# LayerNorm's inverse roots: a GpSimd power and one Newton step on VectorE in place of ScalarE's square root and VectorE's reciprocal

## The chip, the cores and the metric

The kernel runs on one core of a Trainium2 chip. The metric is the device time of one execution in microseconds (us), the median of several runs. The core's engines work side by side, each through its own queue in order: TensorE (PE, with PEld for its weight loads), VectorE (DVE), ScalarE (ACT), GpSimd (POOL) and SyncE (SP, which here only issues DMAs). An engine waits for another through semaphores.

## What is computed

Two pre-LayerNorm layers act on x of 4 x 1024 tokens by 256 features, all in float32. Cut to what matters:

```
def _layernorm(x, eps=1e-05):
    return (x - mean(x)) / sqrt(var(x) + eps)          # over the 256 features

x = x + L0_attn(_layernorm(x))    # causal attention in a window of 64, 16 heads
x = x + L0_ffn (_layernorm(x))    # top 2 of 8 SwiGLU experts, and 2 shared experts
x = x + L1_attn(_layernorm(x))    # full attention; inside it, after the output projection:
                                  #   out = out + input
                                  #   out = (out - mu) * rsqrt(var + 1e-05) * gamma + beta
x = x + L1_ffn (_layernorm(x))    # 8 experts choose 128 tokens each, gates by 8 Sinkhorn rounds
```

So every token has five normalisations: four of the layers, and the one inside the second attention. Each needs one number per token, 1/sqrt(var + eps).

## The kernel before

**Tiles.** A tile is 128 tokens (on the partitions) by 256 features. The 32 tiles `x_t[i]` stay in SBUF from start to end. A unit `u` is four tiles (`UT` = 4), `NT` = 32.

**Statistics and roots.** `note(i)` computes mean and variance of tile i on VectorE (`bn_stats`, `bn_aggr`) into `mv_all[:, i, :]`. `roots(i0, i1)` (L140 to L144) then turns the variances of several tiles at once into inverse roots: ScalarE takes the square root of variance plus epsilon (L143, one column per tile), VectorE the reciprocal (L144), and the result lies in `rstd_all`. ScalarE's functions are kept in tables; a change from a function of one table to one of another shows in the trace as an instruction ACT_TABLE_LOAD. ScalarE computes the softmax exponentials (L378 in layer 0, L1479 in layer 1), the SwiGLU's silu (L725) and plain copies beside the square roots.

**Where roots are taken.**
- At the start for tiles 0 to 3 and 4 to 7, then inside the projection of layer 0 for tiles 8 to 19 (about 31 us) and 20 to 31 (about 235 us). `normalise_steps` uses them in L157 (VectorE), and TensorE transposes the normalised tile `xn` in L164. GpSimd is at the start busy with memsets of the q, k and v buffers (L236, L239, L298).
- For all 32 tiles at the start of layer 0's FFN (about 475 us). In program order GpSimd has there DMA issues (L547, L549, L590, L595), iotas, masks and memsets down to L762, and after them L597, which waits for a DMA.
- For layer 1's attention, for tiles 0 to 3 (about 1204 us), 4 to 11 (about 1268 us) and 12 to 31 (about 1422 us, at the end of `fetches`, which brings the experts' rows back). L1331 in `project` and L1528 in `put_out` use them.
- In `finish` (L1540 and after), ten times, for the inner LayerNorm of one to four tiles (seven times four, then two, one and one): statistics of `y`, root (L1552), reciprocal, then GpSimd applies scale, gamma and beta and adds the result to x (L1559 and after). `note` follows.
- In `gate_steps` (L1014 and after), ten times for the same groups: root (L1017), reciprocal, then GpSimd normalises a tile for the second FFN (L1024), TensorE transposes it and computes gate logits, which VectorE clips (L1055).

**Layer 1's attention loop.** From about 1330 to 2330 us TensorE works step by step. One step computes transposed scores of a head pair into a double PSUM bank (L1471; of its four matmuls two subtract the rows' maxima), scores for later maxima into another (L1429), and sums over values for an earlier step (L1486). ScalarE takes the exp of the first (L1479, 1.02 us) and VectorE the maxima of the second (L1436, 1.2 us). These double banks are one ring of three buffers in turn: a score matmul waits until the exp or the reduction of three buffers earlier has read its buffer.

**Order.** What lies beside the loop (output projections, `finish`, projections of later units, gates, Sinkhorn, choosing tokens, rank DMAs) is written as Python generators. The loop calls `some`, which advances each kind of job by a piece; a `yield 0` or `wait(lag)` in a job gives its turn away, so that other instructions of the same engines come between. The scheduler keeps these instructions behind the newest of the loop's own. `paced` ties GpSimd's fetch DMAs to a ScalarE instruction. The tail after the loop finishes the last tiles with `lag` 0, chooses tokens for the remaining sequences and runs the experts (to 2504 us).

Of the kernel before, what the change touches and what calls it, by code (L numbers as in the profile page):

```python
# [8 lines left out]
F32 = mybir.dt.float32  # L9
# [4 lines left out]
AF = mybir.ActivationFunctionType  # L14
ALU = mybir.AluOpType
# [3 lines left out]
P = 128  # L19
# [3 lines left out]
NT = NB * S // P  # L23
UT = 4
# [9 lines left out]
EPS = 1e-5  # L34
# [5 lines left out]
def two_layers(  # L40
# [33 lines left out]
    nc = tc.nc  # L74
    mm = nc.tensor.matmul

    const = ctx.enter_context(tc.tile_pool(name="const", bufs=1))
    small = ctx.enter_context(tc.tile_pool(name="small", bufs=3))
# [24 lines left out]
    for i in range(NT):  # L103
# [6 lines left out]
    make_identity(nc, ident)  # L110
    identb = const.tile([P, P], BF16, tag="identb", name="identb")
    make_identity(nc, identb)
    eps_t = const.tile([P, 1], F32, tag="eps", name="eps_t")
    nc.vector.memset(eps_t, EPS)

    dsel = const.tile([P, P], F32, tag="dsel", name="dsel")
    nc.gpsimd.memset(dsel, 0.0)
# [1 line left out]
        out=dsel,  # L119
# [12 lines left out]
    mv_all = const.tile([P, NT, 2], F32, tag="mv_all", name="mv_all")  # L132
    rstd_all = const.tile([P, NT], F32, tag="rstd_all", name="rstd_all")

    def note(i: int):
        st = small.tile([P, 6], F32, tag="st", name="st")
        nc.vector.bn_stats(st, x_t[i])
        nc.vector.bn_aggr(mv_all[:, i, :], st)

    def roots(i0: int, i1: int):  # L140

        std = small.tile([P, NT], F32, tag="std", name="std")
        nc.scalar.activation(std[:, i0:i1], mv_all[:, i0:i1, 1], AF.Sqrt, bias=eps_t)  # L143
        nc.vector.reciprocal(rstd_all[:, i0:i1], std[:, i0:i1])  # L144

    def normalise(*args, **kw):
        for _ in normalise_steps(*args, **kw):
# [30 lines left out]
    with ExitStack() as lc:  # L178
# [7 lines left out]
            out=wv_t, in_=w_qkv[:, 2 * D :].rearrange("(k p) e -> p k e", p=P)  # L186
# [3 lines left out]
        with tc.tile_pool(name="a0_raw", bufs=1) as rpool:  # L190
            for n in range(2):
                w_raw = rpool.tile([P, 2, D], F32, name=f"w_raw{n}")
                nc.scalar.dma_start(
                    out=w_raw,
# [3 lines left out]
                for kc in range(2):  # L198
                    for j in range(2):
                        half = slice(j * P, (j + 1) * P)  # L200
# [12 lines left out]
            out=mask_q, in_=mask_q, compare_op=ALU.is_ge, fill=NEG,  # L213
# [3 lines left out]
            out=mask_q, in_=mask_q, compare_op=ALU.is_ge, fill=NEG,  # L217
# [7 lines left out]
            out=spread.rearrange("p (r c) -> p r c", r=4)[:, :, :DH],  # L225
# [8 lines left out]
        for n in range(2):  # L234
# [3 lines left out]
            k = wpool.tile([P, 4, S], F32, name=f"kT{n}")  # L238
# [309 lines left out]
    for b in range(NB):  # L548
        nc.gpsimd.dma_start(  # L549
            out=y_d[b][E * CAP :, :].rearrange("o (p n) -> (o p) n", p=4), in_=none[:4, :]  # L550
# [11 lines left out]
    with ExitStack() as lc:  # L562
# [16 lines left out]
        for n in range(PAIRS):  # L579
            order.append((2 * n, 2, n))  # L580
            if (n + 1) * (NBLK - PAIRS) // PAIRS > n * (NBLK - PAIRS) // PAIRS:
                n = PAIRS + n * (NBLK - PAIRS) // PAIRS
# [181 lines left out]
        for r in range(0, NTILE, 12):  # L764
            n = min(12, NTILE - r)
# [244 lines left out]
    def wait(n: int):  # L1010
        for _ in range(n):
            yield 0

    def gate_steps(i0: int, i1: int, bank, lag: int):  # L1014

        std = small.tile([P, NT], F32, tag="std", name="std")
        nc.scalar.activation(std[:, i0:i1], mv_all[:, i0:i1, 1], AF.Sqrt, bias=eps_t)  # L1017
        yield from wait(lag)
        nc.vector.reciprocal(rstd_all[:, i0:i1], std[:, i0:i1])
        yield from wait(lag)  # L1020
        xns = []
        for t in range(i0, i1):
            xn = gpool.tile([P, D], F32, tag="xng", name="xng", bufs=4)
            nc.gpsimd.tensor_scalar(  # L1024
                xn, x_t[t], mv_all[:, t, 0:1], rstd_all[:, t : t + 1], ALU.subtract, ALU.mult
            )
            nc.gpsimd.dma_start(out=xn_d[t // TB][(t % TB) * P : (t % TB + 1) * P, :], in_=xn)
            xns.append(xn)
            yield 0
        yield from wait(2 * lag)  # L1030
        xTs = []
        for j in range(0, i1 - i0, 2):
            pair = xns[j : j + 2]
            ps = bank()
            for h, xn in enumerate(pair):
                for kc in range(2):
                    c = (2 * h + kc) * P
                    nc.tensor.transpose(ps[:, c : c + P], xn[:, kc * P : (kc + 1) * P], ident)
            xT = gpool.tile([P, 4, P], F32, tag="xTg", name="xTg")
            n = 2 * len(pair)  # L1040
            nc.scalar.copy(xT[:, :n, :].rearrange("p k t -> p (k t)"), ps[:, : n * P])
            xTs += [xT[:, 2 * h : 2 * h + 2, :] for h in range(len(pair))]
            yield 1
        yield from wait(lag)
        ps = bank()
        for j, xT in enumerate(xTs):
            for kc in range(2):
                mm(
                    ps[:, j * E : (j + 1) * E],
                    lhsT=xT[:, kc, :],  # L1050
                    rhs=gw1[:, kc, :],
                    start=(kc == 0),
                    stop=(kc == 1),
                )
        nc.vector.tensor_scalar(  # L1055
            gates[:, i0:i1, :],
            ps[:, : (i1 - i0) * E].rearrange("p (j e) -> p j e", e=E),
            CLIP,
            None,
            ALU.max,  # L1060
        )
        yield 1
# [191 lines left out]
    with ExitStack() as lc:  # L1254
# [285 lines left out]
        def finish(i0: int, ys):  # L1540

            n = len(ys)
            lag = 2 if i0 + n < NT else 0
            mv = small.tile([P, 4, 2], F32, tag="mv1", name="mv1")
            for j in range(n):
                st = small.tile([P, 6], F32, tag="st", name="st")
                nc.vector.bn_stats(st, ys[j])
                nc.vector.bn_aggr(mv[:, j, :], st)
                yield 0
            yield from wait(lag)  # L1550
            std = small.tile([P, 4], F32, tag="std1", name="std1")
            nc.scalar.activation(std[:, :n], mv[:, :n, 1], AF.Sqrt, bias=eps_t)  # L1552
            yield from wait(lag)
            rstd = small.tile([P, 4], F32, tag="rstd1", name="rstd1")
            nc.vector.reciprocal(rstd[:, :n], std[:, :n])
            yield from wait(lag)
            for j in range(n):
                x = x_t[i0 + j]
                nc.gpsimd.tensor_scalar(  # L1559
                    ys[j], ys[j], mv[:, j, 0:1], rstd[:, j : j + 1], ALU.subtract, ALU.mult  # L1560
                )
                nc.gpsimd.tensor_tensor(ys[j], ys[j], gamma_b, ALU.mult)
                nc.gpsimd.tensor_tensor(ys[j], ys[j], beta_b, ALU.add)
                nc.gpsimd.tensor_tensor(x, x, ys[j], ALU.add)
                yield from wait(lag)
            yield from wait(2 * lag)
            for j in range(n):
                note(i0 + j)
                yield 0
            yield from wait(lag)  # L1570
            gating.append(gate_steps(i0, i0 + n, misc_bank, 2 if lag else 0))
            if i0 + n == GT:
                gating.append(share_steps(0, misc_bank, 2))
                gating.append(then(lambda: sort.append(
                    choose_steps(0, misc_bank, chosen, chose)
                )))
# [108 lines left out]
        def fetches():  # L1685

            note_some()
            yield 0
            for i, k in to_fetch:
                fetch(i, k, newest["scalar"])  # L1690
                yield from wait(2)
                take(2)
                note_some()
            yield from wait(4)
            take(0)
            note_some()
            roots(3 * UT, NT)

        def stacks():
            roots(0, UT)  # L1700
# [188 lines left out]
```

## Time and profile before

| | |
|---|---|
| runs | 2508.35, 2501.3, 2497.42 us; median 2501.3 |
| profiled execution | 2505.83 us |
| its span, from the first to the last instruction | 2504.1 us |
| mean granted TensorE clock | 0.955 of full speed |
| ScalarE's table loads | 50 in all, 1.283 us each |
| ScalarE's square roots | 28, about 0.30 us each |

The page gives each engine's busy time and its share of the span; then the span in 40 slices of 62.6 us, each digit being the busy share of a slice in tenths; then groups of instructions (line, engine, operation, output and input, count, busy us, mean ns, idle us of the engine before them and who ended most of it). In the timeline a row gives start and length in us, engine, line, operation, tiles and shapes; a bracket at its end gives the engine's idle time before it and who released it. A row of waits gives the waiting engine and line, who released it, the sum in us, how many times, and the longest.

### The profile page before, as it was taken

How to read it: one execution, taken by the hardware profiler on the slowest of the kernel's cores; microseconds unless marked ns; L12 is line 12 of the kernel's file. 1: busy time of each engine (PE TensorE's matmuls, PEld its weight loads, DVE VectorE, ACT ScalarE, POOL GpSimd, SP SyncE). 2: the span in 40 equal slices, each digit the busy share in tenths (PEclk: the TensorE clock that was granted, in tenths of full speed). 3: DMA queues.
4: the chain of work that ended last, by engine and by line, in shares of the span. 5: the costliest groups of instructions: out<-in, count | busy, mean ns of one | idle time of the engine just before them, and what ended most of it. 6: DMA issues, size and time to landing. Idle time of an engine off the chain costs nothing.

```text
span 2504.1 us, 42234 instructions
## 1 busy us (share of the span) xinstructions
PE 2273.6 (91%) x16844; PEld 1352.2 (54%) x16844; DVE 1392.9 (56%) x2304; ACT 985.6 (39%) x1354; POOL 632.2 (25%) x728
## 2 busy tenths in 40 slices
PE   6999999799999999999888999999999999998434
PEld 3566666566557888887444444444444444443222
DVE  5455545524321222222476877777777798995393
ACT  1333333312111222222114666666666565666311
POOL 2233333510440000000333221212122211124455
PEclk8999999899999999999999999999999999999667
DMA  3000000420116666664515221313121313100144
GB/s 93 19 11 11 11 13 9 133 74 1 66 63 200 217 206 209 213 207 156 117 44 120 59 69 45 69 45 69 45 69 45 69 44 69 44 19 11 56 122 135
DMA packets 201744, 204.90 MB, mean 82 GB/s; under 512 B 90200, under 2 KB 162392, under 8 KB 201548
## 3 DMA queue, kind: packets, MB, share of 16 engines
q1 hardware_dynamic: 179148, 162.13, 22.7%
q0 software_dynamic: 11584, 29.72, 4.0%
q10 hardware_dynamic: 10816, 10.36, 1.2%
q8 instruction: 133, 2.18, 0.4%
q14 instruction: 63, 0.52, 0.1%
HBM read 140.70 MB, written 56.96 MB: 79 GB/s over the span
## 4 chain that ended last, share of the span: by engine, by line
PE 69%; DVE 16%; issue 6%; ACT 4%; POOL 3%; DMA 3%; SPq 0%; DVEq 0%; ACTq 0%; POOLq 0%
PE two L962 10%; PE two L1471 9%; PE acc L1486 8%; PE two L717 6%; DVE tops L1436 5%; PE two L329 5%; PE two L1429 4%; PE acc L989 4%; PE two L258 3%; PE two L1351 2%; PE two L321 2%; PE acc L735 2%; PE misc L735 2%; PE acc L396 2%; PE misc L440 1%
## 5 line engine op out<-in xcount | busy, mean ns | idle before, releaser
L1436 DVE TENSOR_REDUCE tops<-two 128x2 f32<-128x1024 f32 x512 | 619.5, 1217 | 103.8 <-PE two L1429 101.6
L1479 ACT ACTIVATE pT<-two 128x1024 f32<-128x1024 f32 x512 | 523.4, 1025 | 303.7 <-PE two L1471 299.2
L1486 PE MATMUL acc<-pT,v_t 128*32 128x256 f32 x4096 | 342.7, 393 | 5.8 <-ACT pT L1479 5.6
L1471 PE MATMUL two<-q_st,k_st 64*128 64x512 f32 x1024 | 259.8, 499 | 19.3 <-ACT pT L1479 11.8
L962 PE MATMUL two<-xbT,w_t 128*128 128x256 f32 (+1 forms) x1280 | 260.0, 358 | 1.3 <-ACT xbT L951 0.7
L717 PE MATMUL two<-xnT_f,w_t 128*128 128x512 f32 x512 | 234.7, 608 | 7.4 <-DVE tops L1436 5.1
L962 PEld LDWEIGHTS two<-xbT,w_t 128*128 128x128 f32 x1280 | 224.1, 192 | 32.0 <-ACT xbT L951 5.3
L1429 PE MATMUL two<-k_st,q_st 64*128 64x512 f32 x1024 | 220.3, 403 | 4.2 <-DVE glu L726 1.6
L1471 PEld LDWEIGHTS two<-q_st,k_st 64*128 64x128 f32 x1024 | 96.8, 184 | 209.8 <-issue 118.8
L1659 POOL DMA_INDIRECT yr<-ys_d,slot x64 | 62.6, 979 | 573.5 <-DMA w_raw<-in_L_attn_wk_dram 434.7
L1471 PE MATMUL two<-top_st,minus 64*128 64x512 f32 x1024 | 206.5, 396 | 0.0
L978 DVE SCALAR_TENSOR_TENSOR glu_b<-two,b_blk,act_b 128x256 f32<-128x256 f32 (+1 forms) x160 | 72.6, 453 | 235.8 <-ACT act_b L972 235.8
L972 ACT ACTIVATE act_b<-two,b_blk 128x256 f32<-128x256 f32 (+1 forms) x160 | 72.1, 451 | 312.6 <-PE two L962 161.1
L1486 PEld LDWEIGHTS acc<-pT,v_t 128*32 128x32 f32 x4096 | 86.5, 108 | 166.1 <-issue 142.8
L717 PEld LDWEIGHTS two<-xnT_f,w_t 128*128 128x128 f32 x512 | 96.7, 195 | 116.4 <-issue 104.4
L989 PE MATMUL acc<-w_t,glu_b 128*128 128x256 f32 x568 | 148.6, 390 | 8.0 <-DVE glu_b L978 3.7
L355 DVE TENSOR_REDUCE top<-two 128x4 f32<-128x768 f32 (+1 forms) x128 | 112.5, 919 | 69.0 <-PE two L329 69.0
L381 POOL TENSOR_SCALAR_AFFINE_SELECT pT<-pT 128x1024 f32<-128x1024 f32 x64 | 70.5, 1102 | 296.5 <-ACT pT L378 296.5
L725 ACT ACTIVATE act<-two,bT 128x512 f32<-128x512 f32 x64 | 44.0, 687 | 254.0 <-PE two L717 251.2
L1429 PEld LDWEIGHTS two<-k_st,q_st 64*128 64x128 f32 x1024 | 103.2, 185 | 73.5 <-ACT pT L1479 22.0
L378 ACT ACTIVATE pT<-two 128x768 f32<-128x768 f32 (+1 forms) x128 | 93.7, 783 | 119.0 <-PE two L329 118.6
L989 PEld LDWEIGHTS acc<-w_t,glu_b 128*128 128x128 f32 x568 | 102.1, 189 | 34.7 <-DVE glu_b L978 23.3
(317 smaller groups left out, 3095.0 us busy)
## 6 DMA issues: line engine op xcount, KB each, us to landing
w_t<-in_L_ffn_rw_dram SPq DMA_DIRECT2D x120, 512.0 KB
halves<-split SPq DMA_DIRECT2D x64, 256.0 KB
q_st<-halves SPq DMA_DIRECT2D x128, 128.0 KB
k_st<-halves SPq DMA_DIRECT2D x256, 64.0 KB
xb<-xs_d SPq DMA_DIRECT2D x31, 256.0 KB
ys_d<-yb ACTq DMA_DIRECT2D x31, 256.0 KB
xs_d<-zeros SPq DMA_DIRECT2D x5, 1536.0 KB
b_t<-in_L_ffn_rb_dram SPq DMA_DIRECT2D x40, 128.0 KB
```

What stands on the lines that cost most here:

```text
L329: mm(parts[r][:, gg, :], lhsT=left[32 * r : 32 * r + rows, g, l0 : l0 + P], rhs=right[32 * r : 32 * r + rows, g, r0 : r0 + n], start=(mask ...
L355: nc.vector.tensor_reduce(tops[i][:, 2 * ab : 2 * ab + 2, 2 * gp : 2 * gp + 2], scs[ab], AX.X, ALU.max)
L378: nc.scalar.activation(pt[:, 2 * ab : 2 * ab + 2, :, :n], scs[ab], AF.Exp)
L717: mm(ps[:, n * 512 : (n + 1) * 512], lhsT=w_t[:, kc, f * P : (f + 1) * P], rhs=xnT[:, kc, cols], start=(kc == 0), stop=(kc == 1),)
L735: mm(ps[:, jj * D : (jj + 1) * D], lhsT=glu[:, f, j * P : (j + 1) * P], rhs=w3_t[:, f, :], start=(f == 0), stop=(f == NF - 1),)
L962: mm(ps[:, m * 512 + ff * cols : m * 512 + (ff + 1) * cols], lhsT=w_t[:, kc, f * P : (f + 1) * P], rhs=xbT[:, kc, :cols], start=(kc == 0), ...
L989: mm(ps[:, a * D : (a + 1) * D], lhsT=glu[:, f, a * P : (a + 1) * P], rhs=w3_t[:, f, :], start=(f == 0), stop=(f == NF - 1),)
L1429: mm(sc[:, hh], lhsT=q_st[rows, j * P : (j + 1) * P], rhs=k_st[rows, kk * 512 : (kk + 1) * 512], start=True, stop=True,)
L1436: newest["vector"] = nc.vector.tensor_reduce(tops[:, :, j, kk], sc, AX.X, ALU.max).ins
L1471: mm(sc[:, hh * 512 : (hh + 1) * 512], lhsT=minus[rows] if top else k_st[rows, k * P : (k + 1) * P], rhs=(top_ring[p % 2] if top else q_st ...
L1479: newest["scalar"] = nc.scalar.activation(pt, sc, AF.Exp).ins
L1486: newest["tensor"] = mm(oT_ps[32 * r : 32 * r + 32, hh * D : (hh + 1) * D], lhsT=vals[n // HU][:, n % HU, k, :], rhs=pts[r // 2][:, hh * 5 ...
```

## The change

The root is computed without ScalarE. `root_steps` adds epsilon on VectorE (`half`), raises to the power −0.5 on GpSimd, and then makes one Newton step on VectorE: out · (1.5 − 0.5 · half · out²), four small operations. The lag's turns lie between the power and the Newton step. `roots` runs it through at once; `finish`, `gate_steps` and the end of `fetches` run it as part of their generators. The constant tile `eps_t` gives way to `minus_half` (−0.5 in 32 columns). In the new file the lines after this function stand 17 lower at first and 14 lower from `gate_steps` on, roughly.

```diff
-    eps_t = const.tile([P, 1], F32, tag="eps", name="eps_t")
-    nc.vector.memset(eps_t, EPS)
+    minus_half = const.tile([P, NT], F32, tag="minus_half", name="minus_half")
+    nc.vector.memset(minus_half, -0.5)
...
+    def root_steps(out, variances, n: int, lag: int = 0):
+
+        v = nc.vector
+        half, sq = (
+            small.tile([P, 4], F32, tag=f"root{k}", name=f"root{k}", bufs=3)[:, :n]
+            if n <= 4
+            else small.tile([P, NT], F32, tag=f"roots{k}", name=f"roots{k}", bufs=1)[:, :n]
+            for k in range(2)
+        )
+        v.tensor_scalar(half, variances, EPS, None, ALU.add)
+        nc.gpsimd.tensor_tensor(out, half, minus_half[:, :n], ALU.pow)
+        for _ in range(lag):
+            yield 0
+        v.tensor_tensor(sq, out, out, ALU.mult)
+        v.tensor_tensor(sq, sq, half, ALU.mult)
+        v.tensor_scalar(sq, sq, -0.5, 1.5, ALU.mult, ALU.add)
+        v.tensor_tensor(out, out, sq, ALU.mult)
+
     def roots(i0: int, i1: int):
 
-        std = small.tile([P, NT], F32, tag="std", name="std")
-        nc.scalar.activation(std[:, i0:i1], mv_all[:, i0:i1, 1], AF.Sqrt, bias=eps_t)
-        nc.vector.reciprocal(rstd_all[:, i0:i1], std[:, i0:i1])
+        for _ in root_steps(rstd_all[:, i0:i1], mv_all[:, i0:i1, 1], i1 - i0):
+            pass
...
     def gate_steps(i0: int, i1: int, bank, lag: int):
 
-        std = small.tile([P, NT], F32, tag="std", name="std")
-        nc.scalar.activation(std[:, i0:i1], mv_all[:, i0:i1, 1], AF.Sqrt, bias=eps_t)
-        yield from wait(lag)
-        nc.vector.reciprocal(rstd_all[:, i0:i1], std[:, i0:i1])
+        yield from root_steps(rstd_all[:, i0:i1], mv_all[:, i0:i1, 1], i1 - i0, lag)
         yield from wait(lag)
...
             yield from wait(lag)
-            std = small.tile([P, 4], F32, tag="std1", name="std1")
-            nc.scalar.activation(std[:, :n], mv[:, :n, 1], AF.Sqrt, bias=eps_t)
-            yield from wait(lag)
             rstd = small.tile([P, 4], F32, tag="rstd1", name="rstd1")
-            nc.vector.reciprocal(rstd[:, :n], std[:, :n])
+            yield from root_steps(rstd[:, :n], mv[:, :n, 1], n, lag)
             yield from wait(lag)
...
             note_some()
-            roots(3 * UT, NT)
+            i = 3 * UT
+            yield from root_steps(rstd_all[:, i:], mv_all[:, i:, 1], NT - i, 2)
```

## Prediction, made before the changed kernel ran

> **What bounds the kernel now.** I read the shares first, then the slices, the groups, PE's waits, and the timeline at the places that the change touches. On the page:
>
> ```profile
> PE 2273.6 (91%) x16844; PEld 1352.2 (54%) x16844; DVE 1392.9 (56%) x2304; ACT 985.6 (39%) x1354; POOL 632.2 (25%) x728
> ...
> PE   6999999799999999999888999999999999998434
> ...
> DVE  5455545524321222222476877777777798995393
> ```
>
> TensorE carries the kernel. It falls below nine tenths only at the start, at one slice near 470 us, around 1200 us and in the last slices, where chains of small steps decide. Time saved on ScalarE (39%) counts only where TensorE stood still for it. ScalarE's rows, in the groups by line:
>
> ```profile
> L1479 ACT ACT_TABLE_LOAD x19 | 24.4, 1283 | 15.1 <-DVE x L1673 14.8
> ...
> L1552 ACT ACT_TABLE_LOAD x9 | 11.5, 1283 | 0.2
> L1017 ACT ACT_TABLE_LOAD x9 | 11.5, 1283 | 0.2
> ...
> L143 ACT ACT_TABLE_LOAD x6 | 7.7, 1283 | 4.5 <-DMA wv_t<-in_L_attn_W_qkv_dram 4.4
> ```
>
> Each square root in `finish` (L1552) and `gate_steps` (L1017) costs a load, and the next exp (L1479) another. TensorE's longest sum of waits from 1420 to 2340 us is on these exps:
>
> ```profile
> PE two L1471 <- ACT pT L1479: 11.8, 12, 1.1
> ```
>
> One such pair in the timeline (start, length, engine, instruction):
>
> ```profile
> 1479.62 0.50 PE L1471 MATMUL two<-q_st,k_st 64*128 64x512 f32 x2
> ...
> 1480.03 1.28 ACT L1552 ACT_TABLE_LOAD   x1
> 1481.08 0.50 PE L1471 MATMUL two<-q_st,k_st 64*128 64x512 f32 x2
> ...
> 1481.32 0.30 ACT L1552 ACTIVATE std<-mv,eps_t 128x4 f32<-128x4 f32 x1
> ...
> 1481.64 1.28 ACT L1479 ACT_TABLE_LOAD   x1
> 1482.93 2.96 ACT L1479 ACTIVATE pT<-two 128x1024 f32<-128x1024 f32 x3
> 1484.01 0.50 PE L1471 MATMUL two<-q_st,k_st 64*128 64x512 f32 x2 [1.04 <-ACT pT L1479]
> ```
>
> A plain step takes 1.46 us (1479.62 to 1481.08). The exp due at 1480.4 starts at 1482.93, so the next score matmul comes at 1484.01: this step took 2.93.
>
> [...] three L157 took 9.10 us behind GpSimd's memsets (0.3 to 0.4 each elsewhere). [...]
>
> **What goes.** All 28 square roots (0.30 us each) and, as the changed order of ScalarE shows, 45 of its 50 table loads: 45·1.283 + 28·0.30 = 66 us of ScalarE. Most was hidden: plain steps leave it 0.44 us idle each, and TensorE runs ahead. What TensorE gets back, from step periods at each place:
>
> - `finish`: 8 steps of 2.93 against 1.465: 11.8. The pair near 2293 us (2.71 + 1.98 against 2·1.24): 2.2.
> - `gate_steps`: 8 steps of 2.57 against 1.465, 1.1, and 0.2 from a step at L1525 beside it: 8·1.3 = 10.4.
> - The 20 columns at 1422 us: 1.4. The tail after 2325 us: 2.2; its last roots wait on GpSimd's rank DMAs, its iota or the gates' matmuls anyway.
>
> Sum 28.0. Not all of it stays. At 1422 the multiplications stand directly behind the addition on VectorE's order, which then waits out the pow: −1.4. From 1970 to 2290 VectorE is 90% busy with choosing (287.4 of 320 us), and five events there get five small operations instead of one: −2. Near 2309 the context (L1509) stands behind multiplications that wait on a pow behind a DMA issue: −1.2. Left: 23.4.
>
> **What is added.** Per event five VectorE operations, of which the reciprocal's 0.17 is saved: four more of about 0.16 (small operations take 0.155 to 0.19), so +0.5 us net. In the loop a step has about 0.69 us to spare between the maxima's reduction and the next score matmul that needs its buffer, so I cost it at nothing; with that cover gone it would be 16·0.5 = 8. The pow is not in this trace. Smallest POOL operations take 0.13 to 0.16 us (iota, 128x1 and 128x8), which bounds it below[...]. I take between, about 0.06 a column with some 0.2 for each instruction: 0.5, 0.9 and 2[...]. In `finish` two reductions (2·1.2) lie between addition and multiplications, in `gate_steps` more: both hide the pow up to 2.4 us.
>
> GpSimd's queue is what the moved steps pass. At the start:
>
> ```profile
> 10.70 9.10 DVE L157 TENSOR_SCALAR xn<-x,mv_all,rstd_all 128x256 f32<-128x256 f32 x3
> ...
> 16.16 2.85 POOL L298 MEMSET v<- 128x256 f32 x11
> ...
> 19.30 0.66 PE L164 MATMUL misc<-ident,xn 128*128 128x128 f32 x2 [19.30 <-DVE xn L157]
> ```
>
> The changed order has the first pow behind four memsets of 1.80 us (L236, L239, ending 16.2), the second and third behind v memsets. VectorE's additions stand before statistics of later tiles[...]. Then 15 tiles of statistics (0.58 each, 8.7), two L240 copies (2.5), and the multiplications (3·0.3) come ahead of the first xn: first transpose at about 28.7, not 19.3. That is 9.4 lost, less 0.6 for a load gone at 64 us: −8.8. The statistics are moved, not added, so part may be won back later in the stage (TensorE is busy 44.6 of the first 68 us): bounds 0 and −10. At 235 us the pow stands behind L385's select of 1.1 us and VectorE waits for it: −2.2 (bounds 0 and −3.5). At the FFN's start:
>
> ```profile
> 475.45 0.35 DVE L144 RECIPROCAL rstd_all<-std 128x32 f32<-128x32 f32 x1 [0.39 <-ACT std L143]
> 476.39 0.66 PE L164 MATMUL acc<-ident,xn_kept 128*128 128x128 f32 x2 [2.62 <-DVE xn_kept L157]
> ...
> 480.74 0.33 POOL L762 MEMSET zeros<- 128x256 f32 x1
> ...
> 484.50 0.19 DVE L649 TENSOR_TENSOR logits<-acc,gb 128x32 f32<-128x32 f32 x1 [2.43 <-DMA gb<-in_L_ffn_gate_b_dram]
> ```
>
> There the pow stands behind every DMA issue and constant down to L762, so it starts at 481.1; with 2 us of pow and 4·0.19 the roots come at 483.9, not 475.80. TensorE's first transposes follow 7.6 us later than 476.39; the logits wait for gb until 484.50 anyway, with some 2.3 us of slack: −5.3 (bounds −3 and −8.5). Sites at 1204 and 1268 us: their pows follow light work; nothing. SP's order is unchanged and TensorE's nearly so.
>
> **Sum.** +23.4 − 8.8 − 2.2 − 5.3 = 7.1 us gained. The profiled execution took 2505.8 (span 2504.1 and 1.7 around it), 4.5 above the runs' median; it would become 2498.7, and the median 2501.3 − 7.1 = **2494**. Half a per cent, 12.5 us, is about what can be told from no change: faster is below 2488.8, slower above 2513.8.
>
> **Rivals.** *The head costs little (faster).* The start wins its delay back, since statistics done early are not done later, and a quick pow leaves −1 at the FFN: 23.4 − 1.4 = 22 gained, 2479. For it: TensorE's gaps in the first 68 us. Against: the first transpose waits for the whole row of operations, and nothing shows TensorE able to run faster afterwards. *The pow is dear (slower).* Its price c per column meets 76 columns with nothing beside them (12 and 12 in layer 0's projection, 32 at the FFN, 20 at 1422 us). The forecast holds 4.5 us for these; it breaks even at 76·c = 4.5 + 7.1, c = 0.153[...], and is slower by 12.5 from c = 0.32. At c = 0.4 it gives 2501.3 + 18.8 = 2520. From c = 0.6 four columns take 2.4 us and stand out of `finish` too. For it: power has no row here; against: elementwise operations of 128x256 take 0.73 us on GpSimd, 0.003 a column. *The change does not do what it says:* if exps still met other tables the loads would stay; the changed order shows five left, so at most 2% for this, at 2501.
>
> **Chances.** Forecast 0.56 (its own range 2485 to 2503: faster 0.18, same 0.36, slower 0.02); quick head 0.25 (faster 0.23, same 0.02); dear pow 0.17 (slower 0.16, same 0.01); no effect 0.02 (same). Faster 0.41, same 0.41, slower 0.18. The range must reach into both: from 2473 (all of 28 kept) to 2514 (c near 0.32).
>
> **What would show it.** Right: no load at `finish` and `gate_steps`; their steps at 1.47 us; about 28 us less from 1420 to the end before the deductions; first transpose near 28.7, and at the FFN near 484. Wrong: pows of over 2.4 us for four columns, VectorE waiting in the loop for POOL, steps near 1.9 us where the small operations fall, or a first transpose still near 20 us.

## The result, and the profile after

The changed kernel is slower. Six executions took 2511.8 to 2525.1 us, median 2517.5, against 2494.7 to 2508.4, median 2502.4, of the kernel before; the ratio is 1.0067 with a 95% interval of 1.0041 to 1.0092. On another occasion it was 1.0054 (1.0031 to 1.0076). The forecast was 2494, with a range up to 2514. The profiled execution took 2515.85 us, its span 2514.1 against 2504.1.

On the page, the busy times and the slices of TensorE:

```profile
PE 2270.3 (90%) x16844; PEld 1351.9 (54%) x16844; DVE 1409.8 (56%) x2416; ACT 921.3 (37%) x1281; POOL 670.4 (27%) x756
...
PE   5999999699999999999888999999999999998534
```

ScalarE lost 64 us of work, as worked out (66). Its table loads, in the groups by line, are five:

```profile
L742 ACT ACT_TABLE_LOAD x2 | 2.6, 1283 | 11.7 <-DVE xn_kept L174 10.7 <-PE two L734 1.1
L182 ACT ACT_TABLE_LOAD x1 | 1.3, 1283 | 4.4 <-DMA wv_t<-in_L_attn_W_qkv_dram 4.4
L690 ACT ACT_TABLE_LOAD x1 | 1.3, 1283 | 0.0
L1493 ACT ACT_TABLE_LOAD x1 | 1.3, 1283 | 16.5 <-DVE x L1684 16.5
```

So the change does what it says. In exchange GpSimd has the powers. Its groups, kept apart by shape (columns: busy us, mean ns of one, GpSimd's idle time before them):

```profile
L150 POOL TENSOR_TENSOR rstd_all<-root,minus_half 128x4 f32<-128x4 f32 x10 | 10.6, 1058 | 141.9 <-DVE root L149 141.9
...
L150 POOL TENSOR_TENSOR rstd_all<-roots,minus_half 128x32 f32<-128x32 f32 x1 | 5.5, 5472 | 0.0
L150 POOL TENSOR_TENSOR rstd_all<-roots,minus_half 128x12 f32<-128x12 f32 x2 | 4.5, 2262 | 3.1 <-DVE roots L149 3.1
L150 POOL TENSOR_TENSOR rstd_all<-roots,minus_half 128x20 f32<-128x20 f32 x1 | 3.6, 3571 | 11.8 <-DVE roots L149 11.8
```

With 0.57 us for one column, these lie on a straight line: about 0.40 us and 0.158 us a column. The prediction had taken 0.5, 0.9 and 2 us for 4, 12 and 32 columns; they took 1.06, 2.26 and 5.47.

In the loop the exchange works as planned. The timeline of one `finish` (L149 addition, L150 power, L153 to L156 Newton step, L1485 scores, L1450 maxima):

```profile
1494.28 0.16 DVE L149 TENSOR_SCALAR root<-mv 128x4 f32<-128x4 f32 x1
...
1494.51 1.04 POOL L150 TENSOR_TENSOR rstd<-root,minus_half 128x4 f32<-128x4 f32 x1 [12.34 <-DVE root L149]
...
1495.06 0.49 PE L1485 MATMUL two<-q_st,k_st 64*128 64x512 f32 x2
...
1496.53 0.50 PE L1485 MATMUL two<-q_st,k_st 64*128 64x512 f32 x2
...
1497.21 0.15 DVE L153 TENSOR_TENSOR root<-rstd 128x4 f32<-128x4 f32 x1
```

Two reductions hide the power, and the step keeps 1.47 us where before it took 2.93. TensorE's waits for the exps, 11.8 us before, are down to 0.6. The rows of its waits from 1430 to 2345 us for the maxima and for the context show what has grown in their place; before first, after second:

```profile
PE two L1471 <- DVE tops L1436: 6.1, 9, 1.8
PE misc L1038 <- DVE ctx L1509: 3.5, 3, 1.9
```

```profile
PE two L1485 <- DVE tops L1450: 12.0, 12, 3.3
PE misc L1052 <- DVE ctx L1523: 8.8, 3, 7.2
```

To see where the time went, each matmul of one kernel is set against the same matmul of the other. I cut at step 80 of the loop (its score matmul at 1481.1 us before) and at its last step, for two profiled executions of each kernel (`before_look` and `after_again` are the second ones, below):

| us | before, before_look | after, after_again | mean difference |
|---|---|---|---|
| start to step 80 | 1481.1, 1478.3 | 1495.1, 1502.2 | +18.9 |
| step 80 to the last step | 848.7, 848.4 | 846.9, 845.0 | −2.7 |
| last step to the end | 174.3, 176.5 | 172.2, 173.3 | −2.6 |

Ahead of step 80 the offset rises at three places: by 3.7 and 3.3 us at 235 us, by 7.8 and 9.7 at the FFN's start, by 3.1 and 4.5 at 1422 (both profiles of the changed kernel against the first of the kernel before). The loop should have given 21 us and gives 2.7.

The way to step 80 is not the same in every execution: two profiles of one kernel differ there by 2.7 us (before), 7.2 (after) and 13.1 (`linear`, below).

The trace also lists the stretches in which TensorE was granted half its clock, each a multiple of 3.41 us but for the last of a trace. Matmuls of 128x128 in a row (L1341 before, L1355 after) start 0.214 us apart in those of the loop, and 0.11 outside them (medians). I call half the length of the stretches half-clock time: what a TensorE that never waits loses there. From step 80 to the last step it is 8.5 and 8.5 us before, 22.2 and 20.5 after. Without it the loop takes 840.2 and 839.9 us before, 824.7 and 824.5 after: in these executions the waits gave 15.5, and the clock took 12.8 back. In one stretch of the loop of equal length in each kernel, the windows view shows it (busy us of PE, PEld, DVE, ACT, POOL with counts; then the granted clock, DMA share and GB/s); before first, after second:

```profile
1482.00:2223.00 741.00, 718.99 (x6187) 342.40 (x6187) 587.71 (x771) 464.28 (x523) 163.46 (x189) 1.00 0.22 55
```

```profile
1497.00:2238.00 741.00, 726.08 (x6205) 346.30 (x6201) 598.05 (x823) 433.53 (x489) 175.72 (x201) 0.98 0.22 55
```

TensorE is busier, by 7 us in 741, and slower while it is.

### The profile page after: what moved, and what is told of

The parts are those of the page before. It is cut to its first block, busy times and chain, and to the rows that moved or that the text cites. A ratio compares the mean times of both kernels' runs of the same rounds, so it can differ in the third digit from the quotient of the medians.

```text
span 2514.1 us, 42285 instructions
## 1 busy us (share of the span) xinstructions
PE 2270.3 (90%) x16844; PEld 1351.9 (54%) x16844; DVE 1409.8 (56%) x2416; ACT 921.3 (37%) x1281; POOL 670.4 (27%) x756
## 5 line engine op out<-in xcount | busy, mean ns | idle before, releaser
L1450 DVE TENSOR_REDUCE tops<-two 128x2 f32<-128x1024 f32 x512 | 619.4, 1217 | 90.5 <-PE two L1443 88.6
L1485 PE MATMUL two<-q_st,k_st 64*128 64x512 f32 x1024 | 261.1, 503 | 13.1 <-DVE tops L1450 12.0
L1485 PE MATMUL two<-top_st,minus 64*128 64x512 f32 x1024 | 208.9, 399 | 0.0
L1485 PEld LDWEIGHTS two<-q_st,k_st 64*128 64x128 f32 x1024 | 97.3, 185 | 204.2 <-issue 120.1
```

What stands on the lines that cost most here:

```text
L1450: newest["vector"] = nc.vector.tensor_reduce(tops[:, :, j, kk], sc, AX.X, ALU.max).ins
L1485: mm(sc[:, hh * 512 : (hh + 1) * 512], lhsT=minus[rows] if top else k_st[rows, k * P : (k + 1) * P], rhs=(top_ring[p % 2] if top else q_st ...
```

## The experiments

The tables below use these measures: the ratio to the kernel before on the same chip, with its interval; and from the profile, the time from step 80 to step 456 (the loop's middle), the half-clock time in it, and the rest. The expectations name its end step 460, by a count that runs one step further in some kernels than in others; their figures for it differ from these by up to 1 us.

### Each half alone, the ceiling, and the loads put back

`loop_new` has the power and Newton step only in `finish` and `gate_steps`:

```diff
     def roots(i0: int, i1: int):
-        for _ in root_steps(rstd_all[:, i0:i1], mv_all[:, i0:i1, 1], i1 - i0):
-            pass
+        nc.scalar.activation(rstd_all[:, i0:i1], mv_all[:, i0:i1, 1], AF.Sqrt, bias=eps_t)
+        nc.vector.reciprocal(rstd_all[:, i0:i1], rstd_all[:, i0:i1])
...
-            i = 3 * UT
-            yield from root_steps(rstd_all[:, i:], mv_all[:, i:, 1], NT - i, 2)
+            roots(3 * UT, NT)
```

> Power and Newton step only in finish and gate_steps; the roots at the start, at 235, 475, 1204, 1268 and 1422 us are the square root and reciprocal of before (written in place). From the offsets between the two traces the power costs 3.7 us at 235, 7.8 at the FFN's start and 3.1 at 1422, 14.5 in all, and the loop gives back only 1 to 2 us of some 20 because TensorE's clock is halved more often (11 stretches of 3.4 us between 1440 and 2300 us after, 3 before). Theory (the clock takes back what the waits gave): 2497 to 2500, granted clock 0.950 to 0.952. Rival (the extra half-clock stretches are an accident of the profiled execution, the saved waits stay saved): 2483 to 2487, granted clock 0.954 or more.

`heads_new` is the other half, with the old square root and reciprocal in `finish` and `gate_steps` (same two lines, in place).

> The other half: power and Newton step at the six places of roots, square root and reciprocal (in place) in finish and gate_steps. Theory (the power's 0.40 us and 0.158 us a column lie on the path at 235, 475 and 1422 us): slower by 14 to 15 us, 2517, granted clock as before. Rival (the heads' delays are absorbed later and the loop is what slows the changed kernel): 2502 to 2506.

`linear` is the kernel before with

```diff
-        nc.scalar.activation(std[:, i0:i1], mv_all[:, i0:i1, 1], AF.Sqrt, bias=eps_t)
+        nc.scalar.activation(std[:, i0:i1], mv_all[:, i0:i1, 1], AF.Identity, bias=eps_t, scale=0.5)
```

at all three places, and 0.5 in `eps_t`.

> The kernel before with Identity in place of Sqrt on ScalarE (0.5 + 0.5 var, so the roots' values are only near the true ones): 28 activations of 0.3 us and the reciprocals stay, no table loads for roots, no power. It is the ceiling of what the loads can give. Theory (the clock takes back about 12 of 28 us): 2485 to 2489, granted clock near 0.950. Rival (the waits given back stay): 2474 to 2477, granted clock 0.954 or more.

`idle_roots` is the changed kernel with, in `finish` and `gate_steps`,

```diff
+        std = gpool.tile([P, 4], F32, tag="std1", name="std1", bufs=1)
+        nc.scalar.activation(std[:, : i1 - i0], mv_all[:, i0:i1, 1], AF.Sqrt)
         yield from root_steps(rstd_all[:, i0:i1], mv_all[:, i0:i1, 1], i1 - i0, lag)
```

> The changed kernel with an unused square root on ScalarE beside each power in finish and gate_steps, so that the two table loads of each come back, and all else stays. Theory (the waits of the loads let the clock recover): slower than the changed kernel by 6 to 12 us, 2524 to 2530, granted clock back near 0.955. Rival (waits and clock have nothing to do with each other): slower by 20 to 25 us, 2538 to 2543, granted clock 0.951 or below.

Measured (before: median 2507.9 on this chip):

| kernel | median us | ratio | steps 80 to 456 | half-clock time in it | rest |
|---|---|---|---|---|---|
| before (first profile) | | | 742.6 | 3.4 | 739.2 |
| heads_new | 2527.0 | 1.0074 (1.0047 to 1.0100) | 744.6 | 5.1 | 739.4 |
| idle_roots | 2539.1 | 1.0105 (1.0074 to 1.0135) | 747.4 | 8.5 | 738.9 |
| loop_new | 2499.2 | 0.9965 (0.9945 to 0.9985) | 736.1 | 10.2 | 725.8 |
| linear | 2486.1 | 0.9912 (0.9882 to 0.9942) | 736.6 | 11.9 | 724.7 |
| changed kernel (first profile) | | | 739.8 | 13.7 | 726.1 |

The halves part as the theory said. The heads cost 18.6 us (12 to 25), the loop gains 8.8 (4 to 14) and not 20. The last column sorts the kernels by whether the loop has loads: 738.9 to 739.4 with, 724.7 to 726.1 without. `loop_new`, with five small VectorE operations and a power in each event, needs only 1.1 us more there than `linear`, with one reciprocal: these operations are all but hidden. The ceiling of taking all loads away is 22 us (15 to 30), and was 18 (11 to 24) when `linear` ran again below: under my sum of 28 and near the clock theory's 19 to 23.

`idle_roots` divides the two theories. Against the kernel before it is slower by 1.05%, the changed kernel by 0.67%, so the loads brought back cost some 10 us (13 against the second round of the changed kernel, below), near the clock theory's 6 to 12 and about half of what the rival had; but its half-clock time stays at 8.5 us, and its mean clock at 0.945 to 0.951, as the rival had it. The clock needed more runs.

### The changed kernel again, without Newton, with idle powers, and with the FFN's power earlier

`after_again` is the changed kernel.

> The changed kernel once more, on one chip with the next three, for its granted clock beside that of the kernel before. If half-clock time is part of the slowdown (span times one minus granted clock: 127 us against 114 to 119 in the runs so far), it shows 6 to 13 us more of it than the kernel before, and a ratio of 1.004 to 1.008. Rival (that was an accident of chip and runs): the same half-clock time, a ratio of 1.000 to 1.002, as the halves' times without it add to about nothing.

It was 1.0054 (1.0031 to 1.0076). Over all executions the half-clock time of a whole execution (span times one minus granted clock) was 132.1 us, standard error 2.7, against 120.8, standard error 2.0, of the kernel before. The extra 11 us are no accident of one profile. Not all of it is lost time, since a longer gap of TensorE is counted in it too. By the same measure `heads_new`, whose loop is the old one, has 6.3 us more than the kernel before on its chip (standard error 2.5), `loop_new` 5.4 (2.7), and 3.8 (2.2) in its second round below; `linear` has 0.4 (3.5) and 1.0 (2.8). So the 12.8 us of the loop belong to the two profiled executions. As an average they are not shown, and 4 to 5 us is the better estimate from `loop_new`.

`no_newton` drops the four multiplications:

```diff
         for _ in range(lag):
             yield 0
-        v.tensor_tensor(sq, out, out, ALU.mult)
-        v.tensor_tensor(sq, sq, half, ALU.mult)
-        v.tensor_scalar(sq, sq, -0.5, 1.5, ALU.mult, ALU.add)
-        v.tensor_tensor(out, out, sq, ALU.mult)
```

> The changed kernel without the four operations of the Newton step (the power's result is used as it is). Theory (in the loop they fit beside TensorE; on the path they stand at 235, 475, 1268 and 1422 us and at the start, 0.6 to 1.4 us each): 3 to 4 us faster than the changed kernel, its half-clock time unchanged. Rival (VectorE's small operations hold up the choosing phase, where it is 90% busy, and push the clock): 8 to 12 us faster.

Less work, and slower: 2542.0 us, ratio 1.0139 (1.0108 to 1.0170). Both theories missed. At 1200 us it is still 1.1 and 6.1 us ahead of the two profiles of the changed kernel; the loss comes in the loop, at the gates. Its timeline at one of them (L1037 and L1541 are GpSimd's):

```profile
1538.22 1.15 POOL L1037 DMA_DIRECT2D xn_d<-xng  x2
1539.39 0.74 POOL L1541 TENSOR_TENSOR y<-y,rows_b 128x256 f32<-128x256 f32 x1
1540.16 0.42 DVE L1542 TENSOR_TENSOR y<-y,misc 128x256 f32<-128x256 f32 x1 [5.82 <-POOL y L1541]
1540.49 2.35 DVE L1446 TENSOR_REDUCE tops<-two 128x2 f32<-128x1024 f32 x2
1541.77 0.79 PE L1481 MATMUL two<-q_st,k_st 64*128 64x512 f32 x2 [4.48 <-DVE tops L1446]
```

Without a step on VectorE after the power, nothing keeps the gates' four normalisations and DMA issues (L1034, L1037) from standing directly behind the power on GpSimd. They come ahead of the addition of the output bias (L1541). VectorE, which needs that sum, stands still for 5.82 us, the maxima behind it too, and TensorE for 4.48. So this run does not price the Newton step; it shows that its four operations also set GpSimd's order. The row of waits has 30.8 us on the maxima:

```profile
PE two L1481 <- DVE tops L1446: 30.8, 13, 5.3
```

`before_pows` adds to the kernel before, in each `finish` and `gate_steps` with a lag,

```diff
+            for _ in range(2):
+                nc.gpsimd.tensor_tensor(unused, gamma_b[:, :NT], minus_half, ALU.pow)
```

> The kernel before (roots and reciprocals in place) with two unused powers of 128x32 on GpSimd beside each square root of finish and gate_steps in the loop: 32 powers of 5.5 us, 176 us in all, ten times what the changed kernel computes there, and no wait added on the path except that GpSimd's later jobs come up to 11 us later. Theory (a busy GpSimd costs granted clock[...]): half-clock time over 125 us, or VectorE's small operations in these stretches longer than 0.2 us, 2515 to 2530. Rival (neither): within 3 us of the kernel before, half-clock time within 3 us of its.

It took 2702 us, 1.0758. Its groups on GpSimd from 1280 to 1560 us tell why:

```profile
L1020 POOL TENSOR_TENSOR unused<-rows_b,minus_half 128x32 f32<-128x32 f32 x36 | 195.5, 5432 | 4.4 <-DMA rows_b<-in_L_attn_gamma_dram 1.7
```

The powers depended on nothing that is computed in the loop, so the scheduler put all 36 in one row ahead of the loop, and everything behind GpSimd's queue waited 195 us. As a test of the clock it is void.

`ffn_early` calls `roots(0, NT)` right behind the DMA issue of gb instead of behind the memset of zeros.

> The changed kernel with the FFN's roots called right behind the issue of gb's DMA, so that the power stands ahead of GpSimd's constants down to the memset of zeros. Theory (of 7.8 us lost there some 5 are the queue, 3 the power's own 5.5 us and the four operations, less 2 of slack): power starts at 479 instead of 484.2, first transpose of the FFN near 486, 4 to 6 us faster than the changed kernel. Rival (the constants moved behind the power are then late, and the zero fill and weights decide): first transpose as early, but no more than 1 us faster at 530.

The ratio was 1.0044 (1.0025 to 1.0063). The power started 4.6 us after GpSimd's first constant, not 6.9, as DMA issues (L564, L566, 3.4 us) still stood ahead. Across the FFN's start the kernel lost 7.4 us, against 7.8 and 9.7 in the changed kernel and 7.7 in `heads_new`, which has the same code there. Neither theory's size came about, and that the 2.3 us of queue moved out of the way come back is not shown.

### Waits, powers and the clock

`before_waits` and `after_waits` add to each kernel, in every head pair of the loop,

```diff
+            if k == 3 and p < NP:
+                unused = gpool.tile([P, 4], F32, tag="unused", name="unused", bufs=1)
+                nc.scalar.activation(unused, pts[1][:, :4], AF.Sqrt)
```

> The kernel before with one more unused square root of four columns on ScalarE in each head pair of the loop (32, each with its two table loads, placed behind an exp): three times the waits. From the runs so far, steps 80 to 460 take 738.5 to 739.2 us without their half-clock time where the loads are there and 725.7 to 728.8 where they are not, so 24 more pairs there cost about 0.8 us each on average, 20 us or more. Theory (waits of TensorE let the clock recover): half-clock time in steps 80 to 460 falls to 0 to 3.4 us (3.4 to 8.5 with loads so far, 5.1 to 13.7 without). Rival (waits and clock are not tied): 5 to 9 us.

> The changed kernel with the same 32 unused square roots in the loop and no others. Theory (waits let the clock recover): half-clock time in steps 80 to 460 of 3.4 to 7 us instead of 11.9 to 13.7, so the time rises by less than the waits do, by 25 to 35 us against the changed kernel. Rival (not tied): half-clock time of 10 to 14 us, 35 to 45 us slower than the changed kernel.

With them ran a second profile of two kernels.

> A second profile of the kernel before, for the half-clock time of its loop. Theory: steps 80 to 460 again 739 us without their half-clock time, and 2 to 6 us of that. Rival: 8 us or more of half-clock time.

> A second profile of the kernel with the power only in the loop. Theory: steps 80 to 460 again 726 us without their half-clock time, and 9 to 14 us of that. Rival: 2 to 8 us of half-clock time.

Then the power alone, on `linear`, in `finish` and `gate_steps`:

```diff
+        nc.vector.tensor_scalar(half[:, :n], variances, EPS, None, ALU.add)
+        nc.gpsimd.tensor_tensor(unused[:, :n], half[:, :n], minus_half[:, :n], ALU.pow)
```

> The same kernel (Identity in place of Sqrt) with an addition on VectorE and a power on GpSimd, whose result nobody uses, in each finish and gate_steps, as many and as large as the changed kernel has there. If the power costs clock: half-clock time of a whole execution 5 to 8 us above the kernel without it, and 4 to 7 us slower. If the loads' absence does, or neither: within 3 us of it in both, and steps 80 to 460 of 725 to 728 us without half-clock time, as small additions are hidden.

> The kernel before with Identity in place of Sqrt (0.5 + 0.5 var), once more: no loads for roots, no power. Both theories: ratio 0.988 to 0.994. If the loads' absence costs clock: half-clock time in steps 80 to 460 of 9 to 14 us again. If only the power does: 2 to 5 us this time.

> The power only in finish and gate_steps, once more: ratio 0.994 to 0.999, steps 80 to 460 of 726 us without half-clock time.

| kernel | ratio | steps 80 to 456 | half-clock time in it | rest |
|---|---|---|---|---|
| before_look | | 742.4 | 3.4 | 739.0 |
| before_waits | 1.0088 (1.0055 to 1.0121) | 755.5 | 1.7 | 753.8 |
| after_waits | 1.0167 (1.0126 to 1.0208) | 751.1 | 10.2 | 740.8 |
| after_again | 1.0054 (1.0031 to 1.0076) | 738.1 | 11.9 | 726.2 |
| ffn_early | 1.0044 (1.0025 to 1.0063) | 733.0 | 5.1 | 727.9 |
| loop_look | | 735.1 | 8.5 | 726.5 |
| loop_again | 0.9959 (0.9941 to 0.9978) | 732.3 | 5.1 | 727.2 |
| linear_again | 0.9930 (0.9905 to 0.9955) | 735.1 | 10.2 | 724.9 |
| linear_pow | 0.9936 (0.9913 to 0.9960) | 733.5 | 8.5 | 724.9 |

No cost of the power to the clock shows: `linear_pow` has 119.6 us of half-clock time in a whole execution, `linear_again` 118.5 (standard errors 3.0 and 2.4), and the ratio is the same. Nor do waits as such give the clock back: `before_waits` would fit that, but `after_waits` and `idle_roots`, which have loads, contradict it with 10.2 and 8.5 us. So I looked at what stands ahead of each half-clock stretch. In the changed kernel's timeline (first row) and windows (the 3.4 us up to a stretch and the 3.4 us of it, granted clock third from the end):

```profile
1693.55 1.95 PE L1062 MATMUL misc<-gw,xTg 128*128 128x8 f32 x16
```

```profile
1692.50:1695.90 3.40, 3.40 (x34) 2.57 (x32) 1.95 (x4) 1.02 (x1) 0.00 (x0) 0.99 0.04 10
1695.90:1699.30 3.40, 3.40 (x20) 1.55 (x18) 1.23 (x1) 1.48 (x2) 0.60 (x1) 0.51 0.02 5
```

There is no gap: TensorE is busy all 3.40 us. But 1.95 us of it are the gates' 16 matmuls of only 8 columns (L1062). The starts of the stretches lie on a grid of 3.413 us within a profile, all 20 of the first profile before and all 24 of the first after to within 0.03 us; I call the time between two points of it a window. Against that grid I placed all 102 such groups in the loop's middle of the 17 profiles up to here. 62 are followed by a half-clock stretch and 40 are not. The 62 begin in the last 0.12 us of a window or 0 to 1.85 us after its edge; the 40 begin at 1.70 to 3.23. A group of 1.7 us (first to last start) that begins in the first half of a window lies wholly inside it; one that begins later is cut by the edge. So the place of the edge sorts them, and only seven groups, which begin between 1.70 and 1.85, fall either way. By what mechanism the clock falls there, no run shows.

The loads come in through the period. Groups follow each other in `after_again` at 1702.1, 1825.0 and 1948.1 us, 122.9 and 123.1 apart: 36 windows are 122.9, so once a group falls badly, the next mostly does too (5 of 6 in both profiles of the changed kernel). Before, they come at 1560.8, 1684.8, 1810.4 and 1934.4, 124.0 to 125.6 apart, the phase moves on, and 2 of 6 are hit.

The period of 122.9 us contains the half-clock stretch itself. In the nine profiles whose loop has no loads, `no_newton` apart, the first four groups show it: after a group that is hit the next comes 122.8 to 123.2 us later, after one that is not, 121.3 to 121.6. That is 1.3 to 1.6 us short of 36 windows, so a group that escapes puts the next one that much earlier in its window, mostly into the bad half, and from there on the groups are locked, wherever in a window the first one fell (0.04 to 3.03 us). 39 of 54 groups are hit in these profiles. With the loads of before the distances are 125.4 to 125.6 and 123.9 to 124.3, and in five such profiles 12 of 30 groups are hit. The lock can be lost: in `ffn_early`, with the changed kernel's loop, a group slipped out at 1944 us, and 3 of 6 were hit.

The last three kernels take the group apart, tile by tile, each with a turn of its own:

```diff
-        ps = bank()
         for j, xT in enumerate(xTs):
+            ps = bank()
             for kc in range(2):
                 mm(
-                    ps[:, j * E : (j + 1) * E],
+                    ps[:, :E],
...
+            nc.vector.tensor_scalar(gates[:, i0 + j, :], ps[:, :E], CLIP, None, ALU.max)
+            yield 1
```

> loop_new with the gates' logits computed tile by tile, a group of 4 matmuls of 8 columns in a turn of the loop instead of 16 in one, and a clip for each. Theory (16 small matmuls inside one 3.41 us window halve the next window's clock): no half-clock stretch behind a gate group, half-clock time in steps 80 to 460 of 0 to 3.4 us (5.1 to 10.2 before), 4 to 8 us faster than loop_new, ratio to the kernel before near 0.993. Rival (they only coincide): 5 to 10 us of half-clock time, ratio 0.996.

> The same spreading in the kernel before. Theory: half-clock time in steps 80 to 460 from 3.4 to 0 to 1.7 us, ratio 0.997 to 1.000. Rival: no change, or a few us slower from three more clips and turns.

> The same spreading in the changed kernel. Theory: half-clock time in steps 80 to 460 from 11.9 and 13.7 to 0 to 4 us, 8 to 11 us faster than the changed kernel, ratio to the kernel before 1.000 to 1.003. Rival: 10 to 14 us of it, ratio 1.005 to 1.007.

| kernel | ratio | steps 80 to 456 | half-clock time in it | rest |
|---|---|---|---|---|
| loop_spread | 1.0007 (0.9994 to 1.0021) | 737.0 | 0.0 | 737.0 |
| before_spread | 1.0039 (1.0022 to 1.0056) | 748.7 | 0.0 | 748.7 |
| after_spread | 1.0088 (1.0071 to 1.0106) | 739.1 | 1.7 | 737.4 |

The cause holds: in the loop's middle no group is followed by a stretch in any of the three, and the one stretch left there in `after_spread` has no group in the 8 us ahead of it. The time does not hold: the same steps take 10 to 11 us more without their half-clock time, so all that the clock gives is spent. Each tile's matmuls now interrupt a step of their own, and later jobs come up to three turns later; near 2255 us TensorE waits 7.2 us once for the maxima (3.2 at most in `loop_new`):

```profile
PE two L1481 <- DVE tops L1446: 11.5, 9, 7.2
```

How the 10 to 11 us divide among these I did not try.

`loop_new` is the best version, the ceiling apart. In two rounds, each beside the kernel before on one chip, it was faster by 0.35 and 0.41% (9 and 10 us); the changed kernel is 0.5 to 0.7% behind that one.

## Why the prediction was wrong, step by step

Between the 7.1 us gained of the forecast and the 13.6 lost of the profiles lie 20.7. The clock is 12.8 of them, the loop's waits 5.7, the place at 1422 us 3.8, the FFN's start 3.5, the place at 235 us 1.3, and 1.5 have no place; the start was 7.5 and the tail 0.4 better than forecast.

**The removed loads: right in number and place, too dear from 1970 us on.** 45 loads went, and up to 1970 us the steps of `finish` fell from 2.93 to 1.47 us. Outside half-clock time the loop gave 15.5 us against 21.2 in my sum (11.8 + 10.4 + 2.2 − 2 − 1.2). Cut at steps 80, 329 (1970 us before) and 488 (2285 us), with the forecast's terms divided by where their steps lie (of 8 steps in `finish` 4 and 4, of 8 in `gate_steps` 4, 3 and 1):

| us, without half-clock time | before, before_look | after, after_again | linear, linear_again | gain after | forecast |
|---|---|---|---|---|---|
| step 80 to 329 | 485.7, 485.6 | 475.2, 474.9 | 474.8, 474.8 | 10.6 | 11.1 |
| step 329 to 488 | 313.6, 313.3 | 309.5, 309.8 | 308.2, 307.6 | 3.8 | 7.8 |
| step 488 to the last | 40.9, 41.0 | 39.9, 39.9 | 40.1, 39.9 | 1.1 | 2.3 |

The term that failed is the worth of the steps in the second stretch, where VectorE is 90% busy. `linear`, with neither loads nor powers, gains 5.5 us there, so the power and the small operations cost some 1.7, near the −2; but the steps were worth 5.5 and not 9.8. TensorE had waited there for exps only 3.5 us in all, and its waits for the maxima grew from 6.1 to 8.8 (8.1 in `linear`). A step freed of a load met the next wait. (The steps at `gate_steps` are 2.71 to 2.73 us in the trace of before, not 2.57; with the 0.2 beside them the forecast's 1.3 comes out nearly the same.)

**"Near 2309 … −1.2": a longer wait, but not a dearer one.** I had seen the power there behind one DMA issue. In the timeline the power of two columns stands behind the gates' normalisations and their two DMAs:

```profile
2300.70 0.15 DVE L149 TENSOR_SCALAR root<-mv 128x2 f32<-128x2 f32 x1
...
2304.56 1.22 POOL L1041 DMA_DIRECT2D xn_d<-xng  x2
...
2305.79 0.75 POOL L150 TENSOR_TENSOR rstd<-root,minus_half 128x2 f32<-128x2 f32 x1
...
2306.57 0.16 DVE L153 TENSOR_TENSOR root<-rstd 128x2 f32<-128x2 f32 x1 [5.41 <-POOL rstd L150]
```

VectorE stands 5.41 us at L153 with the context (L1523) behind it, and TensorE's waits for the context rise from 3.5 to 8.8 us. That is not 5.3 us lost to the power. `linear`, which has none, waits 7.1 us for the context too:

```profile
PE misc L1038 <- DVE ctx L1509: 7.1, 3, 5.5
```

And the last stretch of the table is as long in `linear` as in the changed kernel. What the power's place costs here is not shown.

**The clock: missing.** The sum took each matmul at the duration that it had before. In the loop of the profiled executions 12.8 us of the gain went to half-clock time. In its middle 6.8 stand behind gate groups, as the shorter period brought five of six into one window instead of two, and 2.6 behind windows in which TensorE was busy for only 1.8 to 2.0 us; 3.4 came at its end, behind longer stalls of TensorE (7.2 us near 2310). It is the largest error of these profiles, and the forecast put it at nothing. In an average execution it is smaller, perhaps 4 to 5 us, as said above, so a part of it is the luck of two profiles; and `linear`, locked like the others, shows next to none over all its executions. What the lock costs on average stays open.

**The power's price: "I take between".** The 0.06 us a column and 0.2 for each instruction were my guess, as no trace of before has a power; measured are 0.158 and 0.40. The FFN's start cost 7.8 and 9.7 us, not 5.3, with the transpose at 491.63 and not near 484:

```profile
484.15 5.47 POOL L150 TENSOR_TENSOR rstd_all<-roots,minus_half 128x32 f32<-128x32 f32 x1
...
491.63 0.66 PE L181 MATMUL acc<-ident,xn_kept 128*128 128x128 f32 x2 [14.46 <-DVE xn_kept L174]
```

**235 us: −2.2, measured −3.7 and −3.3.** The power took 2.27 us, and then the multiplications met GpSimd's selects:

```profile
234.54 2.27 POOL L150 TENSOR_TENSOR rstd_all<-roots,minus_half 128x12 f32<-128x12 f32 x1 [3.14 <-DVE roots L149]
236.77 1.10 POOL L398 TENSOR_SCALAR_AFFINE_SELECT pT<-pT 128x1024 f32<-128x1024 f32 x1
236.84 1.04 DVE L153 TENSOR_TENSOR roots<-rstd_all 128x12 f32<-128x12 f32 x1 [2.38 <-POOL rstd_all L150]
237.92 0.17 DVE L154 TENSOR_TENSOR roots<-roots,roots 128x12 f32<-128x12 f32 x1
238.06 1.10 POOL L402 TENSOR_SCALAR_AFFINE_SELECT pT<-pT 128x1024 f32<-128x1024 f32 x1
238.13 1.06 DVE L155 TENSOR_SCALAR roots<-roots 128x12 f32<-128x12 f32 x1
```

L153 and L155 take 1.04 and 1.06 us instead of the 0.17 that each took on 12 columns at 23.80 and 25.43 us, and end with the select beside them. I read that as held up by it; what holds them, no run shows. I had reckoned with such a hold only at the start. `heads_new` and `ffn_early`, with the same code here, lost 10.8 us each at this place, with 23.9 us of halved clock behind it instead of 6.8; what starts that, no run shows.

**1422 us: net nothing, measured −3.1 and −4.5.** VectorE waits there 3.69 us at L153 for a power of 3.57; I had put that at 1.4.

**The start: −8.8, measured about −1.** The 28.7 rested on my estimate, from the 9.10 us of L157, that the first two additions stop until 16.2 us; they ran at 8.21 and 10.13 with 0.36 and 0.41 us. Nor did the statistics come after the memsets: they ran beside them at 0.39 us each and were done at 16 us. The first transpose came at 24.82, 5.5 later than before, not 9.4:

```profile
24.82 0.66 PE L181 MATMUL misc<-ident,xn 128*128 128x128 f32 x2 [24.82 <-DVE xn L174]
```

And at 231 us the offset was 0.0 and 2.5 us. The statistics done early were not done later. That lower bound of 0 was in the text, and the quick-head rival had the reason.

**The rivals.** The dear power was right on the price, c = 0.158, and by its own sum that gives 76·0.158 − 11.6 = +0.4 us, no change. Price alone does not make 15 us. With measured terms: heads −17.4 (start −1.3, 235 us −3.5, FFN −8.8, 1422 us −3.8, each the mean of two profiles), waits in the loop +15.5, its clock −12.8, tail +2.6, and −1.5 ahead of step 80 that no place accounts for, most of it from the 2.7 us by which the second profile of the kernel before is ahead of the first: −13.6, against 10 to 15 lost in the medians.

## What to carry to other kernels

A wait that is taken off the busiest engine is worth its step period only while no other wait ends close behind it and that engine's clock stays (here the steps from 1970 us on gave 5.5 us and not 9.8, and the clock of two profiles took 12.8); read the granted clock by stage, from more than one profile, and look at what the engine did in the window before it fell. An operation that moves to another engine's queue costs what stands ahead of it there, and its price by column decides where it belongs: here four columns beside a loop cost some 2 us in 16 events and 12 to 32 columns at a stage's start cost 3 to 10 each. Before a short chain is shortened, look at what it keeps apart: four small operations held GpSimd's order.

## What the runs showed of the hardware

- A power on GpSimd took about 0.40 us and 0.158 us a column of 128 partitions: 0.57 us for one, 5.47 for 32.
- Behind 62 of 102 groups of 16 matmuls of 8 columns (1.7 us from first to last start, TensorE busy throughout) the granted clock was half in the next window of 3.41 us: these began in the last 0.12 us of a window or up to 1.85 us after its edge. Behind the 40 that began at 1.70 to 3.23 it was not (17 profiles), nor behind any group taken apart tile by tile (three profiles).
- Two VectorE operations on 12 columns, each beside a GpSimd select of 1.10 us, took 1.04 and 1.06 us; the two that started between and behind the selects took 0.17 each.
